# One-hot matrices with the experts innermost and 16-bit operands, and a new order of the operations, in a layer of two mixtures of experts and a state-space scan

## The chip, the cores and the metric

The kernel runs on one core of one Trainium2 chip. The metric is the device time of one execution in microseconds (us), as a median of several runs. The core has five engines that run side by side, each with its own queue of instructions taken in order: TensorE (PE; its weight loads are listed apart as PEld), VectorE (DVE), ScalarE (ACT), GpSimd (POOL) and SyncE (SP), which issues most of the DMAs. An instruction that must wait for another engine holds up everything behind it on its own engine.

## What is computed

The input x has 2 sequences of 2048 positions with 128 features, in float32. Three stages follow one another, each added to x:

```python
x = x + 0.5 * ffn(layernorm(x))     # mixture of experts
x = x + attn(layernorm(x))          # state-space scan
x = x + 0.5 * ffn(layernorm(x))     # mixture of experts, the same weights
```

The mixture `ffn` takes all positions as one flat list of tokens and treats each of them by itself.

```python
scores = softmax(flat @ router_w.T + router_bias)       # 32 experts
topk_scores, topk_idx = top_k(scores, 4)                # normalised to a sum of 1
h = silu(flat @ gate_w[e].T) * (flat @ up_w[e].T)       # per expert e, 128 wide
out = sum over the 4 experts of score * (h @ down_w[e].T)
out = out + (silu(flat @ sgate_w.T) * (flat @ sup_w.T)) @ sdown_w.T   # shared, 512 wide
```

The scan `attn` computes, from the 128 features, 256 channels u, z and dt and 16-wide B and C per position, and then for each position t in order

```python
h = h * exp(dt_t * A) + (dt_t * u_t) * B_t     # 256 channels x 16 states
y_t = sum over the states of h * C_t  + D * u_t
```

followed by `y * silu(z)` and a projection back to 128 features. Position t needs the state of position t-1, so the blocks of one sequence follow one another.

## The kernel before

The 4096 positions are 8 blocks (`NBLK`) of 512 (`T`), four to a sequence; a block is a tile of 128 partitions x 4 (`TB`) x 128. Blocks 0 to 3 are one sequence, 4 to 7 the other. Each mixture is done in four groups of blocks (`GROUPS`, line 37): in the first layer blocks (0), (1), (2, 3), (4 to 7), in the second (0 to 3), (4, 5), (6), (7). The text names them M00 to M03 and M10 to M13, and the scans of the blocks S0 to S7.

**A group of several blocks** sorts its tokens by expert with indirect DMAs: POOL writes ("scatters") each token's row four times, once for each of its experts, into a table in HBM (L964), the experts' quads read it back, and POOL fetches ("gathers") the four results of every token (L1347). Behind every third such DMA in a row a POOL memset of `pad` (L406) lets time pass.

**A group of one block** (M00, M01, M12, M13; `fixed` in the code) sorts without DMAs. The token rows are split in three 16-bit parts (`xp`), and a one-hot matrix `oh` says which token stands in which place of which expert's tile of R rows (`ROWS`: 96 rows, in M13 112). `loc` (L1010) holds for each token and expert the place within that expert's tile; `marks` (L1159) compares it with the numbers 0 to R-1 in `iota_s`, two of the four token tiles at a time; `sorted_rows` (L1173) multiplies, 12 matmuls a quad, into the PSUM tile `pt_x`. A group has 8 quads of 4 experts (`SQ`), so 16 `marks` and 96 such matmuls. Then, for all groups alike, ACT copies `pt_x` to `xT` (L1184), PE makes gate and up (`gu`, L1192), ACT the silu (L1204), DVE the product `h` (L1210), PE the down product (`oq`, L1220), ACT copies it to `yq` (L1229), SP stores it. After the last quad of a group stands the operation `more` on all engines (L1275): a branch that is not taken when all tokens found place. Behind it come the gathers and their weighted sum into x (`joined`, L1372, or matmuls, L1404).

**The scan** of a block has 16 steps, one for each state: POOL makes the driving term (L1630), ACT two decays (`da`, L1642), DVE two scans over 512 positions (L1668) and the product with C (L1681), PE turns and sums (L1445).

**The order.** Every piece of work is declared with `op(engine, cost, function, reads, writes, ...)`, 4233 in all, numbered as they are declared. `Plan.run` does not plan: it takes the order written out in the string `ORDER`, and checks it against the dependences and against the rings of buffers (`RINGS`). The operations are emitted in that order, so each engine's queue follows from it. `tables` (L410) loads another function table on ACT (L412) wherever a silu follows an exponential in this order or the reverse: 140 such loads before.

```python
for part in ORDER.split():
    first, _, last = part.partition("-")
    order += [self.ops[i] for i in range(int(first), int(last or first) + 1)]
```

The weights of the experts are read from the inputs once, in M00, and laid into `w_dram` in HBM from there; rows of tables that may stay unwritten are cleared at the start (L478).

Of the kernel before, what the change touches and what calls it, by code (L numbers as in the profile page):

```python
# [9 lines left out]
BF16 = mybir.dt.bfloat16  # L10
# [38 lines left out]
0 93-96 3 492 97-98 2 10 8 120 491 493 9 121-122 99-101 264 494 102-106 123 495-496 108 107 109 497 11 110-111 13 12  # L49
557 559 558 560 112 561 563 124 113 562 262 16 29 23 564 116 500 114 177 565 60 567 1 115 117-118 566 568 266-267 50  # L50
24 501-502 14 42 119 182 569 571 498 503 268-269 504 499 19 18 570 59 181 505-506 183 273 64 21 572 274 164 28 573 165
179 300 507-508 47 275 509 184 301 166 37 72 145 574 510 65 27 55 511 167 30 302 512 25 40 143 125 127 185 514 513 45
186-187 20 515 86 126 128 516 129 270 160 22 131 130 188 26 271-272 15 517 189 17 525 529 551 265 132 147 548 58 190
148 550 69 518 133 135 263 276 134 136 149 277 180 199 137 150 521 144 168 198 162 139 138 171 169-170 554 215 140
172-173 216 200-201 519-520 191 535 178 154-155 141 522 192 156 303 523 7 5 524 575 211 304 142 228 819 577 6 151 305
152 161 306-307 576 153 174 327 53 175 579 233 578 194 217 278 581 196 580 52 213 4 532 232 218 157-158 308 583 44 57
821 556 193 820 31 582 250 249 205 214 328 585 206-207 163 555 542 547 584 309 546 549 202-203 586-587 234 204 534 589
176 235 310 543 146 526 311-312 247 230 588 590 818 536 822 552 823 208 591-592 540 209 197 313-314 316 332 537 334
219 222 210 553 220-221 333 528 545 223-224 335 315 239 317-318 240 245 241 251 319-320 323 252 212 225 824 336 195
226 527 338 256 159 539 76 257 54 258 337 339 236-238 340 342 253 324 538 341 533 254-255 343 325 231 242 246 531 56  # L60
243 229 530 248 344 244 331 259 227 46 260-261 345-346 279 825 36 347 834 348 541 39 326 544 829 826 91 930 932 43 292
329 349 931 830 290 831 933-934 428 827 330 41 936 828 935 835 937 836 938 832 352 427 940 839 833 939 941 353 321 942
322 34 943 33 49 944-945 840 837-838 841 35 593 842 48 843-846 848 850 849 847 851 85 32 350 298 282 285 852-853 855
854 856-858 63 429 51 283 351 354-355 38 288 649 430 398 395 425 431-433 281 61 75 410 396 287 356 397 357 412 291 413
358 426 411 399 359-361 434 400 435-436 367 297 368 414-415 437 404-405 438 362 296 406 366 458 363 419-420 439 74
369-370 401-402 421 280 293 284 416 68 295 457 417-418 365 403 459-460 407 286 866 408 885 455 371-373 380 461-462 867
422 456 364 409 463 423 79 90 878 374-375 442 376-377 381 440 83 594 382 464 82 378 383 441 465 384-385 289 294 859
893 389-390 466 876 424 467 896 386 468 299 443 877 873 892 747 387 391 62 444 388 596 1395 595 445 597 886 446-447
1396 875 449-450 874 887 451 448 598 601-603 607 599 868 872 890 379 600 392-393 469 650 652-654 1397 651 608 80 895
869 897 894 452 81 453 677 880 891 889 879 881 655-656 604-605 657-659 609 882 862 888 863 1398-1402 84 883-884 870  # L70
1404 394 454 470 678-679 1403 871 1405 1415-1416 1421-1424 1417-1418 660-661 1419 1425 680-682 489 685 1420 610 748
473 476 683 1426 918 903 684 686 611 687 77 1408 78 1409-1413 750-751 864 662 615-616 1429 1414 617 749 755 92 1431
1430 1427 688 483 471 1433 612 1432 689 1434 663 613 606 756 67 757 752-753 1439-1440 614 1435 1441 618 666 1449 1436
905 481 1459 619 1443 667 1442 664 754 758 668 691 1444-1445 1450 472 482 1460 665 929 912 1451 636 669 692 690 1437
759 1452 1454 1446 1455 1453 1456 1461 635 1428 1438 1448 638 1447 671 1464 1463 1462 1465 1469-1470 1479 670 1457
1466 694 1471 693 1472 695 734 637 474 639 672 1474 640-641 487-488 1473 720 673-674 1481 1458 620 642 1475 643 1476
910 1482 1468 675 696-697 733 736 66 1480 1484-1485 1483 1467 1491 719 1478 1489 698 1492 1486 644 1493 1477 479 486
478 475 1499 737 760 645 1406 1490 920 699 1407 700 1494-1495 738 646-647 739 1496 1501 477 1487 621 484 904 480
701-702 676 1502 740 703 722-723 1500 1504 1488 1511 1505 485 724 721 725-726 1497 735 741 909 914 922 921 727-728
1503 1506 1509 705 742-743 1519 490 1510 1513-1514 1512 729 1498 648 706 744 708 1521 745 1599 73 71 1515 70 1600 704  # L80
730 1516 709 1508 1518 917 926 906 928 622 1522 1520 1524-1525 731 1601 1523 1529 1602 761 707 713 1603 732 1526 710
714 1533 711-712 746 899 915 900 913 1531-1532 715 860-861 624-625 1530 1604 626 623 1507 1539 908 1605 627 629 924
902 1534-1535 1003-1004 630 628 716 1017 631 898 1528 1540 1549 1517 1608-1609 923 919 1559 927 916 717 1541 1073 632
1542 633 1550 1536 718 1538 1537 865 1543 901 1610 1606-1607 1611 1544 1551 1545-1546 1612-1613 1615-1616 1554 1553
1018 1527 907 1614 1552 925 911 634 1569 1555 1625-1626 1617-1618 1561 1031 1627 1560 1619 1548 1562 1628 1556 88 1016
1002 1570 1563 1620 762 1564 1621-1622 1629 1030 1558 1557 1019 1571 1565 1005 1547 1623-1624 1074 1020 1072 1574 1021
1032 1572 1006 1010 1024 1022 1566-1567 1579 771 1573 1023 1086 1011 1025 1012 1075-1076 766 1580 769 1033 764 1034
1633 1026 1044 1007-1008 1575 1077-1078 1576 1009 1079 1027 1581 1058 1643 1028 1013-1014 1630 1038 1080 1045 1035
1584 89 1583 1568 1039-1040 1081 1029 1082 786 1036-1037 1059 1046-1047 1582 1585 1048 1635 1634 1083-1084 1041-1042
1061 1089 1586 765 1636 1090 1062 1101 1060 1644 1100 1638 1087 1639 1578 1049-1051 773 1052 1066 1102 1053 1067 763  # L90
1015 1103 1054 1068 1645 1637 1653 1640 1648 1646 1577 1104 772 1588 1055-1056 1649 1088 1663 767-768 770 1085 1655
1091 1114-1115 1092 1647 1063-1064 1093 1065 1650 1108 778 1654 1589 1594 1109 1094 1105 776 1587 783 1631 1043 1095
1106 1656 806 1110 1673 1657 1069 1664 1128 1096 1683 1107 1057 1658-1659 1070 1651 777 1665 1097-1098 1117 1632 780
1118 1641 1660 1111 1131 1642 1112 1666 779 784 1667 1132 1156 1668-1669 774-775 1675 785 1116 1142 1159 1119 1129
1071 1122 1160 1157 1130 1670 1661 1120 1123 1652 1693 781 787 1671 1121 1674 1143 1158 1124 1677 788 1678 1145 782
1676 789 1803 1146 1804 1685 1703 1595 1662 1596 1144 1805 1679 1684 1688 1184 1680 1125 1694 1185 1136 793 1126 1686
1133 1164 1713 807 1672 1689 1704 1165 1723 1134 1687 1137-1138 1682 1695 1166 1806-1807 1186 1696 1135 1690 1150 1161
1810 1127 1198 1099 1698-1699 1162 1151 1811 1692 1681 1697 1152 1163 1705 1590 1706 1139 1187 1140 1188 1691 1700
1591 1701 1113 1714 1733 1708 1167 1702 1709 791 1724 1707 1710 1715 1168 1141 1718 1808 1170 1192 1171 87 1716 1147
1809 798 1743 1193-1194 799 1201 1717 1173 1734 1148-1149 1199 1719-1720 1816 1725 1728 1727 1712 1202 1726 1817 1819  # L100
1153 800 1172 1820 1174 1753 1729 1203 1722 1735 1821 1154 1736 1822 1721 804 1204 792 1178 1763 1730 1738 1731 1205
1179 1737 1180 1200 1206 1711 1207 1739 1189-1190 1175 1732 1176 1745 1208 1740 1191 1744 1754 1177 1748 1829 1746
1749 1747 1830 1818 1773 1755 797 1831 1758 1756 790 1750-1751 1741 1832 1759 1592 1226 1593 1764 1169 1765 1823-1824
1742 1212 805 1757 1752 1195 1213 1783 1254 1766 1825 1227 1768 1760 1214 1826 801 1597 1774 1767 1833 1837 1784 1761
1155 1196-1197 1598 1769 1827 1847 1209 1215 1228 1775 1834 1778 794 1210 1776 1857 1762 1181 1216 1182 1779 1770 1785
# [209 lines left out]
def macaron_kernel(  # L315
# [243 lines left out]
    for R in sorted(set(ROWS.values())):  # L559
# [5 lines left out]
        steps_of[R] = cut, head, n  # L565
    iota_s = kept("iota_s", [P, P])
    nc.gpsimd.iota(iota_s.t, [[1, P]], channel_multiplier=0, allow_small_or_imprecise_dtypes=True)
    iota_p = kept("iota_p", [P, 1])
    nc.gpsimd.iota(iota_p.t, [[0, 1]], channel_multiplier=1, allow_small_or_imprecise_dtypes=True)


# [1258 lines left out]
```

## Time and profile before

| | |
|---|---|
| time before, median of 3 runs (lowest to highest) | 1249.62 us (1238.38 to 1252.58) |
| the profiled execution: its own time | 1252.94 us |
| its span, from the first to the last instruction | 1251.2 us |
| mean granted TensorE clock | 0.899 of full speed |
| busy: PE, DVE, POOL, ACT | 950.7, 931.3, 903.8, 751.8 us |
| `marks`, all 64 | 61.7 us of DVE |
| function table loads, 140 | 179.6 us of ACT, 1283 ns each |

"Busy" is the time in which an engine ran an instruction. The page's second part cuts the span into 40 slices of 31.3 us and gives the busy share of each in tenths. A group of instructions is listed with its line, engine, operation, tiles (written<-read), shapes, count, busy time and mean duration, and behind the bar the idle time of its engine just before these instructions and what ended it. A wait is put down to the engine whose work came last.

### The profile page before, as it was taken

How to read it: one execution, taken by the hardware profiler on the slowest of the kernel's cores; microseconds unless marked ns; L12 is line 12 of the kernel's file. 1: busy time of each engine (PE TensorE's matmuls, PEld its weight loads, DVE VectorE, ACT ScalarE, POOL GpSimd, SP SyncE). 2: the span in 40 equal slices, each digit the busy share in tenths (PEclk: the TensorE clock that was granted, in tenths of full speed). 3: DMA queues.
4: the chain of work that ended last, by engine and by line, in shares of the span. 5: the costliest groups of instructions: out<-in, count | busy, mean ns of one | idle time of the engine just before them, and what ended most of it. 6: DMA issues, size and time to landing. Idle time of an engine off the chain costs nothing. (4 is left out here: it accounts for less than half of the span.)

```text
span 1251.2 us, 18918 instructions
## 1 busy us (share of the span) xinstructions
PE 950.7 (76%) x5752; PEld 730.4 (58%) x5752; DVE 931.3 (74%) x1798; ACT 751.8 (60%) x1390; POOL 903.8 (72%) x917
## 2 busy tenths in 40 slices
PE   5978687666779898776878735757787887899883
PEld 3756465456578686454646524544576766677552
DVE  7863853289678899999999999998873465776533
ACT  4443324685879899977898755646676553533120
POOL 0483584588777786899979788888638476778576
PEclk9998889797889999998998877777899998999987
DMA  9884766394679764232432312223499767766432
GB/s 305 279 257 160 214 191 187 107 289 157 197 236 280 222 196 135 69 84 59 101 77 62 79 52 74 82 86 87 139 309 283 217 210 227 241 194 192 144 99 68
DMA packets 211117, 207.93 MB, mean 166 GB/s; under 512 B 21697, under 2 KB 179522, under 8 KB 210978
## 3 DMA queue, kind: packets, MB, share of 16 engines
q1 hardware_dynamic: 196642, 176.92, 46.9%
q0 software_dynamic: 14336, 29.39, 8.2%
q8 instruction: 59, 0.97, 0.3%
q14 instruction: 80, 0.66, 0.2%
HBM read 146.26 MB, written 59.97 MB: 165 GB/s over the span
## 5 line engine op out<-in xcount | busy, mean ns | idle before, releaser
L1630 POOL TENSOR_TENSOR hst<-dtu,bs 128x1024 f32<-128x1024 f32 x128 | 302.6, 2369 | 90.2 <-DMA bs<-bd 30.1
L1347 POOL DMA_INDIRECT yg<-ys,idx x192 | 190.0, 990 | 93.7 <-issue 37.7
L1668 DVE TENSOR_TENSOR_SCAN hst<-da,st,hst 128x512 f32<-128x512 f32 x192 | 240.2, 1272 | 23.5 <-ACT da L1642 10.3
L1192 PE MATMUL gu<-xT,wt 128*128 128x128 f32 (+2 forms) x1536 | 209.9, 289 | 40.8 <-DMA wt<-w_dram 9.7
L1192 PEld LDWEIGHTS gu<-xT,wt 128*128 128x128 f32 x1536 | 196.3, 202 | 65.2 <-issue 29.9
L1642 ACT ACTIVATE da<-dt,a 128x512 f32<-128x512 f32 x256 | 174.5, 689 | 79.4 <-DVE hst L1668 73.9
L1445 PEld LDWEIGHTS y<-ident,hst 128*128 128x128 f32 x1024 | 133.9, 156 | 108.3 <-issue 78.1
L1445 PE MATMUL y<-ident,hst 128*128 128x128 f32 x1024 | 150.3, 298 | 46.6 <-DVE hst L1681 44.8
L964 POOL DMA_INDIRECT xs<-xn,idx x128 | 128.2, 1002 | 77.9 <-DVE hs L1045 44.3
L1210 DVE TENSOR_TENSOR h<-sgq,gu 128x256 f32<-128x256 f32 (+2 forms) x192 | 72.9, 396 | 146.4 <-ACT sgq L1204 79.9
L412 ACT ACT_TABLE_LOAD x140 | 179.6, 1283 | 3.3 <-PEq L1818 0.8
L1681 DVE TENSOR_TENSOR hst<-hst,c 128x1024 f32<-128x1024 f32 x128 | 154.7, 1209 | 5.1 <-PE c L1654 2.2
L1204 ACT ACTIVATE sgq<-gu 128x256 f32<-128x256 f32 (+2 forms) x192 | 67.2, 367 | 120.0 <-PE gu L1192 76.8
L1220 PE MATMUL oq<-wt,h 128*128 128x128 f32 (+2 forms) x768 | 115.4, 298 | 27.0 <-DVE h L1210 12.6
L1220 PEld LDWEIGHTS oq<-wt,h 128*128 128x128 f32 (+2 forms) x768 | 102.3, 200 | 48.3 <-DVE h L1210 14.2
L1184 ACT COPY xT<-pt_x 128x512 f32<-128x512 f32 (+2 forms) x96 | 52.9, 555 | 81.5 <-PE pt_x L1173 39.3
L1229 ACT COPY yq<-oq 128x512 f32<-128x512 f32 (+2 forms) x96 | 55.8, 582 | 67.8 <-PE oq L1220 45.4
L1654 PE MATMUL c<-cm,pick 128*128 128x512 bf16 x128 | 53.4, 417 | 51.5 <-DVE hst L1681 48.3
L1347 POOL DMA_INDIRECT yg<-xs,idx x64 | 65.4, 1023 | 33.8 <-issue 21.1
L406 POOL MEMSET pad<- 128x256 bf16 x268 | 87.9, 328 | 0.2
L1668 DVE TENSOR_TENSOR_SCAN hst<-da,hst 128x512 f32<-128x512 f32 x64 | 75.6, 1211 | 12.1 <-POOL hst L1630 7.0
L964 POOL DMA_INDIRECT xs<-dtu,idx x64 | 65.4, 1023 | 24.5 <-DVE idx L880 13.0
(175 smaller groups left out, 1636.0 us busy)
## 6 DMA issues: line engine op xcount, KB each, us to landing
wt<-w_dram SPq DMA_DIRECT2D x256, 192.0 KB
bs<-bd SPq DMA_DIRECT2D x128, 256.0 KB
xs<-xs SPq DMA_DIRECT2D x64, 256.0 KB
wt<-w_dram SPq DMA_DIRECT2D x32, 384.0 KB
xs<-zero SPq DMA_DIRECT2D x40, 256.0 KB
ys<-yq SPq DMA_DIRECT2D x40, 256.0 KB
w_dram<-wt SPq DMA_DIRECT2D x16, 384.0 KB
xs<-yq SPq DMA_DIRECT2D x24, 256.0 KB
```

Source lines behind the costliest of these rows:

```text
L406: pool(nc.gpsimd.memset(pad, 0.0))
L412: nc.scalar.preload_act_table_set(name)
L964: nc.gpsimd.indirect_dma_start(out=xs_b.t, out_offset=bass.IndirectOffsetOnAxis(ap=route["idx"][:, i * TB + t, k : k + 1], axis=0), in_=xn ...
L1192: nc.tensor.matmul(gu.t[:, j, s, :], wt.t[:, s, j * H : (j + 1) * H], xT.t[:, s0 + s, :], start=True, stop=True,)
L1210: lambda h=h, s0=s0, sg=sg, gu=gu: nc.vector.tensor_tensor(h.t[:, s0 : s0 + 2, :], sg.t, gu.t[:, 1, :, :], ALU.mult),
L1220: nc.tensor.matmul(o.t[:, s, :], h.t[:, s, :], wts[s // 2].t[:, s % 2, 2 * H :], start=True, stop=True,)
L1347: nc.gpsimd.indirect_dma_start(out=yg.t[:, k, :], out_offset=None, in_=ys_t, in_offset=bass.IndirectOffsetOnAxis(ap=route["idx"][:, i * TB ...
L1445: nc.tensor.matmul(y[:, t, k * P : (k + 1) * P], src[:, k, t * P : (t + 1) * P], ident.t, is_transpose=True, start=start and k == 0 and t ...
L1630: nc.gpsimd.tensor_tensor(h.t[:, :, 1:], dtu.t, bs.t.unsqueeze(1).to_broadcast([P, ND, T]), ALU.mult)
L1642: nc.scalar.activation(da.t, dt.t[:, k, :], AF.Exp, scale=a_t.t[:, k, s : s + 1])
L1668: nc.vector.tensor_tensor_scan(h.t[:, k, 1:], da.t, h.t[:, k, 1:], 0.0 if ini else st_sb[:, k, s : s + 1], ALU.mult, ALU.add,)
L1681: nc.vector.tensor_tensor(h.t[:, :, :T], h.t[:, :, 1:], cb.t.unsqueeze(1).to_broadcast([P, ND, T]), ALU.mult,)
```

## The change

The one-hot matrix is laid out anew. In `oh` the four experts of a quad are now the innermost dimension and the rows stand outside them (`[P, TB, P, SQ]` in place of `[P, TB, SQ, P]`). The numbers that `loc` is compared with come from a new 16-bit constant `rows_s`, 4 equal numbers for each row, written once by POOL at the start; `loc` itself is written as 16-bit. So both operands of `marks` are bf16 and run with step 1 over the innermost four, where before both were f32 and the second stood still over the innermost R. The matmuls of `sorted_rows` therefore give their columns by row and then expert; the tile `pt_x` is kept in that order, and ACT's copy to `xT` now reads it with a step of 4 elements, to write the same `xT` as before. The `more` branch keeps the old layout.

`ORDER` is replaced throughout. Its numbers name the same 4233 operations.

```diff
 ORDER = """
-0 93-96 3 492 97-98 2 10 8 120 491 493 9 121-122 99-101 264 494 102-106 123 495-496 108 107 109 497 11 110-111 13 12
+...
-...
+4088-4090 4216 4221 4226 4231-4232
 """
...
+    rm = max(ROWS.values())
+    rows_s = kept("rows_s", [P, rm, SQ], BF16)
+    nc.gpsimd.iota(
+        rows_s.t, [[1, rm], [0, SQ]], channel_multiplier=0, allow_small_or_imprecise_dtypes=True
+    )
...
-            xp, loc = buf("z", [P, 3, TB, D], BF16, name="xp"), buf("loc", [P, TB, E])
+            xp = buf("z", [P, 3, TB, D], BF16, name="xp")
+            loc = buf("loc", [P, 2, TB, E], BF16, part=lambda t: t[:, 0])
...
-            px = buf("w", [P, SQ, R], name="pt_x")
+            px = buf(
+                "w", [P, SQ, R], name="pt_x",
+                part=(lambda t: t.rearrange("p s r -> p (s r)").rearrange("p (r s) -> p s r", s=SQ))
+                if fixed else None,
+            )
...
-                oh = buf("dt", [P, TB, SQ, P], BF16, name="oh", part=lambda t: t[:, :, :, :R])
+                oh = buf("dt", [P, TB, P, SQ], BF16, name="oh", part=lambda t: t[:, :, :R, :])
...
                         nc.vector.tensor_tensor(
                             oh.t[:, t0 : t0 + 2],
-                            iota_s.t[:, :R].unsqueeze(1).unsqueeze(1).to_broadcast([P, 2, SQ, R]),
+                            rows_s.t[:, :R, :].unsqueeze(1).to_broadcast([P, 2, R, SQ]),
                             loc.t[:, t0 : t0 + 2, q * SQ : (q + 1) * SQ]
-                            .unsqueeze(3)
-                            .to_broadcast([P, 2, SQ, R]),
+                            .unsqueeze(2)
+                            .to_broadcast([P, 2, R, SQ]),
                             ALU.is_equal,
                         )
...
                             nc.tensor.matmul(
-                                px.t,
+                                px.t.rearrange("p s r -> p r s"),
                                 xp.t[:, j, t, :],
                                 oh.t[:, t],
```

## The prediction

> **What bounds the kernel now.** I read the page's slices first, then its stretches, then who waits for the operation that the change makes faster, last the chain at the end. The slices, each 31.3 us:
>
> ```profile
> PE   5978687666779898776878735757787887899883
> DVE  7863853289678899999999999998873465776533
> ACT  4443324685879899977898755646676553533120
> ```
>
> DVE is full from slice 11 to slice 28: there the scans run. Before and behind it DVE is half idle and PE is fuller. So I cut the span at the first scan (246 us), at the first scan of the last block (848) and at its last one (1030), and asked for each engine's busy time in each stretch (columns: stretch, length, then busy us and count of PE, PEld, DVE, ACT, POOL, and last the clock, DMA share and GB/s):
>
> ```profile
> 0.00:246.00 246.00, 183.94 (x1012) 132.06 (x1013) 140.54 (x483) 104.31 (x205) 126.65 (x196) 0.90 0.68 213
> 246.00:848.00 602.00, 444.62 (x2671) 346.02 (x2670) 544.98 (x765) 467.46 (x863) 507.19 (x369) 0.89 0.46 134
> 848.00:1030.00 182.00, 146.68 (x981) 120.24 (x980) 119.14 (x211) 115.10 (x186) 118.32 (x130) 0.93 0.69 210
> 1030.00:1252.00 222.00, 175.49 (x1093) 132.09 (x1091) 126.59 (x340) 64.97 (x137) 151.59 (x225) 0.91 0.57 167
> ```
>
> The opening is 246 us with DVE idle for 105; the scans are bound by DVE (545 of 602); the last 222 us by PE more than by DVE, which is idle for 95. Now `marks`, by shape, and the answer for its line on who waited for it:
>
> ```profile
> L1159 DVE TENSOR_TENSOR oh<-iota_s,loc 128x768 bf16<-128x768 f32 x48 | 44.8, 948 | 0.0
> L1159 DVE TENSOR_TENSOR oh<-iota_s,loc 128x896 bf16<-128x896 f32 x16 | 16.9, 1085 | 1.4 <-issue 1.0 <-PE pt_x L1173 0.3
> ```
> ```profile
> who waited for it (us, times):
>   PE pt_x L1173: 0.9, 1
> ```
>
> All 64 lie in the two outer stretches, 32 in each, where DVE has room. Only once, for 0.9 us, did PE wait for one. What a shorter `marks` can give must come through the DVE instructions queued behind it.
>
> **Part 1, the faster comparison.** The two shapes give its price: 128 elements more take 137 ns more, 1.07 ns an element, with 948 - 768 x 1.07 = 126 ns fixed. The trace of before has no DVE product of two 16-bit operands, so I bound it: at worst nothing is gained (948 and 1085 ns stay; more elements or bytes are not moved, so no loss); at best two elements go where one went, 126 + 411 = 537 and 126 + 479 = 605 ns. I take the best end, because the shapes' rows say that four fifths of the duration is per element; it saves 0.41 us and 0.48 us: 32 x 0.41 = 13.2 us of DVE in the opening, 16 x 0.41 + 16 x 0.48 = 14.3 us in the last stretch, none in between.
>
> [...]
>
> How much of it is on the path? It can give no more than what PE waits for DVE behind the first `marks`. The waits of PE between 28 and 246 us that name DVE, the longest of them:
>
> ```profile
> PE tot L791 <- DVE mk L779: 8.3, 1, 8.3
> ...
> PE gu L1192 <- DVE x L1068: 4.4, 1, 4.4
> ...
> PE pt_x L1152 <- DVE ea L1584: 3.7, 1, 3.7
> PE oq L1220 <- DVE h L1210: 3.1, 3, 1.3
> ```
>
> With `h` for `gu` (1.0) and `oh` (0.9) that is 21.4 us. Before the 8.3 us DVE runs the routing of M03, with four `marks` among it from 126 to 133 us (4 x 0.41 = 1.6), but much of that stretch is itself a wait for PE's `up`; `ea` has no `marks` ahead of it. I take 4 us of the 13.2. In the last stretch PE waits for DVE 4.1 (`oq` for `h`) + 3.5 and 2.9 (for x L1372) + 1.5 (`hs`) = 12.0 us; the x of L1372 wait for gathers, so mainly the `h` can shrink: 3 us of the 14.3. Ends: 0 and 13.2, 0 and 12.0. Nothing covers what is left over: it becomes idle time of DVE.
>
> **Part 2, the copy.** ACT now reads `pt_x` with a step of 16 bytes, 32 times (480 ns for 384 elements before). No row shows a strided read of PSUM. The nearest is DVE's strided write `mk` (L779): 304 ns at 128 elements, 1.24 us at 512 with the wider step, where a plain 512 takes 0.69. So between 0 and as much again, 32 x 0.5 = 16 us of ACT, which is idle for 142 us of the opening and 157 of the end; but PE waits 10.4 (weight loads) and 7.7 us (matmuls) for all 96 copies together, so a third of the worst case, 5 us, would come through. I take 0. `rows_s` is one more iota on POOL (iota_s took 227 ns for 128 elements, so about 0.8 us), at 2 to 3 us, when POOL then sits idle until 48 us: nothing. `sorted_rows` keeps its counts and streams.
>
> **Part 3, the order.** I set the two orders side by side, engine by engine. The stages keep their places. Adding up the DVE durations of this trace along each queue (neighbours overlap a little, so the sums exceed busy time): from the first scan of S0 to the last of S6 584.2 us of DVE work before and 587.7 after; within S7 131.5 and 126.8; behind the last scan 160.4 and 148.6, of which 14.3 is part 1. So DVE's queue changes by about 1 us between the first scan and the last. On PE one `gate_up` and one `down_q` of M02 leave the stretch ahead of the first scan: eight matmuls each, 1.03 + 1.04 = 2.1 us. Behind the last scan PE has two `gate_up`, a shared `gp` and one turned y more, about 5 us, and SP and DVE nothing of weight. On POOL seven scatters of M02 now stand behind M00's first gathers; those wait for `more` (until 116 us before), so the scatters land 10 us later on a POOL that before sat idle twice, 19.6 and 13.0 us, and their rows are first used by PE at 193 us. Hidden; without that cover it would be 10 us. On SP the first weights of M00 stand behind about 3 MB more of loads and clears (twelve transfers of 256 KB); at the 373 GB/s of the second ten us they land 8 us later. Before they are issued from 3.4 us on and first used by PE's `gu` at 33.5 us, so I take 0 of the 8.
>
> The function table loads rise from 140 to 152: +1 ahead of the first scan, +7 in S0 to S6, +6 in S7, -2 behind. A load and the next instruction:
>
> ```profile
> 223.41 1.28 ACT L412 ACT_TABLE_LOAD   x1
> 224.71 0.58 ACT L1577 ACTIVATE ps_dt<-ps_dt 128x512 f32<-128x512 f32 x1
> ```
>
> so 12 x 1.283 = 15.4 us of ACT. [...] Here the next instruction starts 0.02 us behind the load, so the trace decides for 1.283. Between 246 and 848 ACT is idle for 134 us, 74 of them (over the whole run) waiting for DVE to free a buffer of its decays; the loads fit into that, and I cost them at 0.
>
> What else the new order does with single waits cannot be counted. Downward: DVE idles between 246 and 848 for `h` on ACT 12.4 us, for POOL's driving term 11.4, for decays 8.9, without a named cause 7.8, for `cm` 3.5: 44 us; half of it gone would be -22. Upward: all twelve loads on the path, +15.4. I take -2, the PE work that left the opening, since it is the only row that I can count.
>
> **Sum:** -4 - 3 - 2 = -9 us, so 1252.94 - 9 = 1244 us for an execution like the profiled one. That one lies 3.3 us above the median of the runs, 1249.62; the median so becomes **1240.6 us**, 0.7% less.
>
> **Rivals.** (a) *Nothing gets through:* the 0.9 us that PE waited for `oh` speaks for it, the waits of 21.4 and 12.0 us against. Then 1249.6, and with the copy's 5 us 1255. (b) *The order gives more:* part 1 at its ends, -13.2 - 12.0, or half of DVE's scan waits, -22, with the -9: 1249.6 - 31 = 1219 to 1228. For it: 57 us of DVE idle time in the scans; against: the same work stands between the same scans. (c) *Slower, by the table loads:* in S0 to S7 ACT runs 41 to 47 of 50 us between 350 and 500 us, and DVE already waits for its decays; a load put directly ahead of a decay delays a scan by 1.28 us. All 13 that are new from S0 to S7: +16.7 with nothing gained, 1266 us. It becomes slower by over 1% once ten of them (12.8 us) are on the path. [...]
>
> **How the numbers follow.** A measurement of this kernel can tell about 1% from no change: 1237.1 to 1262.1 is "same". The forecast's own range is 1229 to 1246 and has 0.5, of which 0.22 lie below 1237; (a) and (d) 0.15; (b) 0.15; (c) 0.20. So faster 0.37, same 0.43, slower 0.20. The range takes in most of (b) and all that (c) gives up to ten or so loads: 1217 to 1265; two in ten are left out.
>
> **What would show it.** Right: `marks` at about 540 and 605 ns; the copy of 384 elements still at 480; 152 loads at 1283 ns; the first scan near 241 us and the stretch from there to the last scan within 5 us of 783. Wrong: `marks` unchanged; copies near 700 ns; DVE's idle time for decays above 8.9 us by tens (c); the first scan before 232 us or the scan stretch shorter by over 15 (b). If the opening shrinks but the end does not move, the gain was given back to PE.

## The result, and the profile after

| | before | after |
|---|---|---|
| median (lowest to highest), same chip | 1250.03 us (1238.38 to 1252.58), 4 runs | 1261.37 us (1255.05 to 1269.13), 4 runs |
| ratio, with its 95% interval | | 1.0117 [1.0067, 1.0166] |
| the profiled execution: its time, its span | 1252.94, 1251.2 us | 1255.05, 1253.3 us |
| `marks`, all 64 | 61.7 us | 35.9 us |
| table loads | 140, 179.6 us | 152, 195.0 us |

The change made the kernel slower by 1.2%. The profiled execution of after is its fastest, that of before its slowest, so the two traces differ by only 2 us; what they show is where time moved. The slices of after (31.3 us each):

```profile
PE   5988777575789888677786756656787877999874
DVE  6854742487578899899999999987775355774443
ACT  4544325787789798878798856636757653542220
```

DVE is less busy at the start, as forecast. Slices 15 to 27, all at 9 before, now hold an 8 at 17 and at 27, and 28 to 30 show 7, 7, 7 for 8, 8, 7: while the scans run, DVE is less full. The stretches, cut at the same places of the work as in the prediction (columns: stretch, length, busy us and count of PE, PEld, DVE, ACT, POOL, then clock, DMA share and GB/s):

```profile
0.00:239.00 239.00, 184.90 (x1011) 132.94 (x1011) 128.80 (x483) 105.16 (x206) 123.95 (x197) 0.92 0.71 220
239.00:856.00 617.00, 448.04 (x2684) 349.92 (x2684) 540.81 (x772) 477.84 (x871) 508.63 (x376) 0.89 0.45 128
856.00:1037.00 181.00, 142.71 (x936) 116.77 (x935) 108.26 (x201) 118.23 (x185) 118.26 (x131) 0.93 0.70 213
1037.00:1253.00 216.00, 175.67 (x1125) 134.90 (x1125) 114.56 (x343) 67.57 (x141) 147.30 (x225) 0.93 0.59 174
```

The opening is 7 us shorter, the last stretch 6. In the second line, from the first scan on, the scans S0 to S6 take 617 us where they took 602, with *less* DVE work (541 for 545): DVE stands idle there for 76 us instead of 57. `marks`, ACT's copy and the table loads, by shape:

```profile
L1170 DVE TENSOR_TENSOR oh<-rows_s,loc 128x768 bf16<-128x768 bf16 x48 | 26.2, 559 | 3.1 <-PE pt_x L1184 1.0 <-PE gp L1037 0.9 <-issue 0.8
L1170 DVE TENSOR_TENSOR oh<-rows_s,loc 128x896 bf16<-128x896 bf16 x16 | 9.7, 618 | 1.2 <-PE pt_x L1184 1.2
L413 ACT ACT_TABLE_LOAD x152 | 195.0, 1283 | 3.6 <-PEq L1829 0.8
L1195 ACT COPY xT<-pt_x 128x384 f32<-128x384 f32 x24 | 11.4, 477 | 36.7 <-PE pt_x L1184 21.6 <-PE oq L1231 7.1 <-remote 3.8
```

The comparison is as fast as estimated (559 and 618 for 537 and 605 ns), and the copy with its step of four elements costs what it cost (477 for 480 ns). What DVE waited for in the second stretch, before (246 to 848 us) and after (239 to 856 us): who waits and for whom, us in total, times, the longest:

```profile
DVE h L1210 <- ACT sgq L1204: 12.4, 11, 3.2
DVE hst L1668 <- POOL hst L1630: 11.4, 8, 4.3
DVE hst L1668 <- ACT da L1642: 8.9, 13, 1.7
...
DVE hst L1681 <- PE c L1654: 2.2, 3, 1.8
```
```profile
DVE hst L1679 <- POOL hst L1641: 23.7, 18, 3.6
DVE h L1221 <- ACT sgq L1215: 14.5, 15, 3.6
DVE hst L1679 <- ACT da L1653: 9.8, 13, 2.2
DVE hst L1692 <- PE c L1665: 4.0, 8, 0.8
DVE z L1746 <- PE pz L1735: 3.7, 1, 3.7
...
DVE x L1426 <- PE sum L1415: 2.2, 2, 2.0
```

The scans' wait for POOL's driving term has doubled (+12.3 us), and four others (for `sgq`, `c`, `pz`, `sum`) have grown by 2 to 4 us each; the wait for `cm` (3.5 us before) is gone. The decays (`da`), by which the forecast's rival (c) would show, account for 0.9.

Of the 12.3 us, 9.4 fall into S0 (2.7 to 12.1 us), a block that now begins earlier: the scans of its first state end at 242.1 us for 252.7, those of S1's at 363.6 for 368.2. From there to the same point of S7 it takes 493.3 us where it took 482.9, and in this part the wait for POOL has hardly grown (7.5 to 8.5 us).

### The profile page after: what moved, and what is told of

Same layout as the page of the kernel before. It is cut to its first block, busy times and chain, and to the rows that moved or that the text cites. A ratio compares the mean times of both kernels' runs of the same rounds, so it can differ in the third digit from the quotient of the medians.

```text
span 1253.3 us, 18990 instructions
## 1 busy us (share of the span) xinstructions
PE 951.3 (76%) x5752; PEld 734.5 (59%) x5752; DVE 892.4 (71%) x1798; ACT 768.8 (61%) x1402; POOL 898.1 (72%) x926
## 5 line engine op out<-in xcount | busy, mean ns | idle before, releaser
L1679 DVE TENSOR_TENSOR_SCAN hst<-da,st,hst 128x512 f32<-128x512 f32 x192 | 239.6, 1272 | 23.2 <-POOL hst L1641 11.4
L1203 PE MATMUL gu<-xT,wt 128*128 128x128 f32 (+2 forms) x1536 | 215.7, 294 | 45.8 <-issue 12.9
L1203 PEld LDWEIGHTS gu<-xT,wt 128*128 128x128 f32 x1536 | 200.8, 206 | 72.5 <-issue 23.3
L413 ACT ACT_TABLE_LOAD x152 | 195.0, 1283 | 3.6 <-PEq L1829 0.8
L1692 DVE TENSOR_TENSOR hst<-hst,c 128x1024 f32<-128x1024 f32 x128 | 155.1, 1212 | 13.6 <-remote 5.9
L1231 PE MATMUL oq<-wt,h 128*128 128x128 f32 (+2 forms) x768 | 110.1, 290 | 13.4 <-DVE h L1221 8.2
L407 POOL MEMSET pad<- 128x256 bf16 x276 | 90.9, 329 | 0.2
L1358 POOL DMA_INDIRECT yg<-xs,idx x64 | 62.2, 972 | 29.5 <-DVE x L1383 13.5
L1037 PE MATMUL gp<-xnT,w_all 128*128 128x512 f32 x128 | 72.0, 646 | 13.2 <-issue 8.0
```

The source lines that it names most:

```text
L407: pool(nc.gpsimd.memset(pad, 0.0))
L413: nc.scalar.preload_act_table_set(name)
L1203: nc.tensor.matmul(gu.t[:, j, s, :], wt.t[:, s, j * H : (j + 1) * H], xT.t[:, s0 + s, :], start=True, stop=True,)
L1231: nc.tensor.matmul(o.t[:, s, :], h.t[:, s, :], wts[s // 2].t[:, s % 2, 2 * H :], start=True, stop=True,)
L1358: nc.gpsimd.indirect_dma_start(out=yg.t[:, k, :], out_offset=None, in_=ys_t, in_offset=bass.IndirectOffsetOnAxis(ap=route["idx"][:, i * TB ...
L1679: nc.vector.tensor_tensor_scan(h.t[:, k, 1:], da.t, h.t[:, k, 1:], 0.0 if ini else st_sb[:, k, s : s + 1], ALU.mult, ALU.add,)
```

## The experiments

**Theory Q** (called O in the first four expectations): the new order costs the time, through waits of DVE between the first scans of S0 and S5 that it had not before. **Rivals:** L, the twelve added table loads cost it; the layout costs it (called L, too, in the first two expectations); P and C, what a faster comparison gives is lost in the outer stretches, where PE and the clock it is granted set the pace.

The kernel before takes 1204, 1246, 1268 and 1272 us on the other chips that these runs got, so only ratios to it on the same chip are compared, and stretches that depend on the chip only within a chip. Since the operations are the same, any two orders can be joined wherever the dependences and rings of buffers allow it. The table has the medians' ratios and, from each one's profiled execution, the time up to the scans of S0's first state ("opening"), from there to the same point of S7, then to S7's last scan, and the rest of the span.

| kernel | before on its chip | ratio [95%] | opening | S0 to S6 | S7 | rest |
|---|---|---|---|---|---|---|
| before / after (the result) | 1250 | 1.0117 [1.0067, 1.0166] | 252.7 / 242.1 | 598.4 / 614.9 | 178.1 / 179.8 | 222.0 / 216.6 |
| marks_only | 1204 | 0.9951 [0.9924, 0.9979] | 231.7 | 597.9 | 163.6 | 207.0 |
| order_only | 1204 | 1.0133 [1.0087, 1.0179] | 220.7 | 617.0 | 166.2 | 209.4 |
| ends_new | 1204 | 0.9947 [0.9919, 0.9975] | 221.5 | 610.4 | 164.0 | 198.2 |
| mid_new | 1204 | 1.0133 [1.0086, 1.0180] | 229.6 | 614.4 | 164.9 | 203.8 |
| marks_relu | 1272 | 1.0676 [1.0610, 1.0742] | 268.2 | 585.3 | 273.0 | 227.8 |
| after_relu | 1272 | 1.0780 [1.0731, 1.0830] | 263.7 | 610.1 | 265.0 | 240.3 |
| win_s2_s4 | 1272 | 1.0205 [1.0152, 1.0258] | 272.6 | 614.5 | 187.9 | 228.0 |
| win_s5_s6 | 1272 | 1.0119 [1.0064, 1.0173] | 268.2 | 595.9 | 188.0 | 234.3 |
| before_same_chip | 1246 | one time, 1245.3 us | 247.7 | 597.5 | 180.0 | 218.4 |
| after_same_chip | 1246 | 1.0106 [1.0072, 1.0141] | 240.7 | 617.6 | 177.0 | 219.1 |
| marks_same_chip | 1246 | 1.0022 [0.9992, 1.0051] | 251.0 | 596.7 | 179.2 | 226.1 |
| ends_same_chip | 1246 | 1.0035 [0.9998, 1.0072] | 242.3 | 608.7 | 177.8 | 223.8 |
| marks_twice | 1268 | 1.0250 [1.0205, 1.0295] | 268.0 | 597.4 | 186.6 | 246.5 |
| loads_28 | 1268 | 1.0132 [1.0089, 1.0175] | 256.1 | 607.4 | 187.0 | 231.6 |
| s2_old | 1268 | 1.0186 [1.0134, 1.0237] | 263.3 | 608.4 | 179.1 | 243.2 |
| one_move | 1268 | one time, 1295.6 us | 262.8 | 617.2 | 180.8 | 233.2 |
| marks_third | 1246 | 1.0057 [1.0018, 1.0097] | 254.5 | 590.6 | 181.0 | 220.6 |
| layout_f32 | 1246 | 0.9992 [0.9957, 1.0027] | 244.2 | 600.4 | 177.9 | 218.0 |

(The last two are a further chip, 1245.75 us.)

### 1. The layout alone, the order alone, and the order by halves

```diff
 marks_only: the code of after
-ORDER = new
+ORDER = old
 order_only: the code of before
-ORDER = old
+ORDER = new
 ends_new: the code of after
-ORDER = new
+ORDER = new up to S0's first scan, old up to S7's first scan, new behind it
 mid_new: the code of after
-ORDER = new
+ORDER = old up to S0's first scan, new up to S7's first scan, old behind it
```

> The new layout of the comparisons (experts innermost, 16-bit operands, the strided copy) with the order of before kept as it was. Theory O (the order costs the time, between the first and the last scan): this kernel gains the forecast's parts 1 and 2 alone, 1240 to 1247 us against 1250. Theory L (the layout costs it, by the strided copy or by a clock that falls when PE is fed faster): 1255 to 1263. By both the comparisons take about 559 and 618 ns.

> The layout of before with the order of after. Theory O: the order's loss without the layout's gain, 1264 to 1272 us. Theory L: 1245 to 1250, as the forecast's part 3 alone. Under both the table loads are 152.

> The new layout; the order of after up to the first scan of S0 and from the first scan of S7 on, the order of before in between (144 table loads). Theory O with the loss between the scans S0 to S6: 1238 to 1246 us, so faster than before. If the loss lies in the opening or in the tail instead: 1252 to 1263.

> The reverse: the new layout; the order of before up to the first scan of S0 and from the first scan of S7 on, the order of after in between (148 table loads, the eight new ones all in S0 to S6). Theory O with the loss between the scans: 1254 to 1264 us. If the loss lies at the ends: 1238 to 1246.

The ratios fall in two pairs: the old order in the middle gives 0.995, the new one 1.013, whatever the ends and the layout are. So the order of the middle costs 1.8%, some 20 us by the medians and 16.5 us by the stretch S0 to S6 (597.9 to 614.4). mid_new's 1.0133 is a little above its expectation (at most 1264 us for 1250, 1.011). Of the 16.5 us, 13.4 arise behind S1's first scans, which end at 346.9 and 347.9 us. The order of the ends is worth nothing. The opening does get 10 us shorter with it (231.7 to 221.5); but S0 to S6 then takes longer by 12.5, although the order there is the old one: 4.2 of it in S0, and 6.5 in S6, where the order is cut.

### 2. Without table loads, and where in the middle

```diff
 marks_relu, after_relu
-SILU = "silu_and_others"
+SILU = "natural_log_exp_and_others"
-AF.Silu
+AF.Relu
 win_s2_s4: marks_only's
-ORDER = old
+ORDER = old up to S2's first scan, new up to S5's first scan, old behind it
 win_s5_s6: likewise, from S5's to S7's first scan
```

> Left out: the SiLU. Every Silu is a Relu, which needs no function table of its own, so that no table is switched; else this is marks_only (new layout, order of before). It gives the price of its 139 switches: fully hidden 1196 us as marks_only, fully on the path 1196 - 139 x 1.283 = 1018. I expect 1110 to 1170. It is the base for after_relu.

> Left out: the SiLU, as in marks_relu; else the changed kernel, its order included. Against marks_relu this is the order's cost without any table switches. Theory L (the twelve added table loads cost the time): equal to marks_relu within 5 us. Theory Q (the order of the queues costs it by its waits, loads or not): 12 to 22 us above marks_relu.

> marks_only, but with the order of after from the first scan of S2 up to the first scan of S5. By the stretches of marks_only and mid_new (S2 +6.7, S3 +1.3, S4 +2.7 us) 1204 to 1211 us if theory Q holds and the loss is here. By theory L the three loads that are new here give 4 us: 1200 at most.

> marks_only, but with the order of after from the first scan of S5 up to the first scan of S7. By the stretches of marks_only and mid_new (S5 -1.7, S6 +3.5 us) 1195 to 1200 us under either theory (two new loads); more than 1204 would mean that the loss is not where the stretches of single executions put it.

With the Relu one table load is left (1283 ns in marks_relu). The time as a whole went up, where I had expected 1110 to 1170 us, for a reason of its own: the branch `more`, skipped otherwise, runs 112 matmuls, presumably since the changed values send more rows past the fixed tiles, and S7 takes 273 us. Up to S7 the pair is clean: 585.3 with the old order, 610.1 with the new one. **Without any table switch the new order still costs 24.8 us** there (14 us by the medians); theory L as the cause has fallen. Of the 24.8 us, 12.5 fall into S0, which begins 4.5 us earlier, 6.4 into S1 and 2.8 into S2: other blocks lose than with the switches (section 3). Against win_s5_s6, which has the old order up to S5 on the same chip, 88 loads fewer gained 10.6 us, 0.12 us a load, far from 1.283.

win_s2_s4 puts S2 to S4 at 231.4 us where the old order has 216.5 (win_s5_s6): +14.9 (7.9 of it in S2), where theory Q had 10.7; by the medians it is 10.1 us slower than win_s5_s6. The new order in S5 and S6 costs nothing there (175.6 us; the old order has 174.7 in marks_relu and 175.5 in marks_only). But win_s5_s6's ratio is 1.012, not below 1, and win_s2_s4's 1.021, not 1.000 to 1.006. Since S0 to S6 take 595.9 us in win_s5_s6, as with the old order elsewhere, the miss must lie in the outer stretches; no profile of the kernel before was taken on this chip. That led to the next runs.

### 3. Everything on one chip

> The kernel before, unchanged, for a profile from the same chip as the next three runs, since absolute times differ between the chips seen so far (1204, 1250, 1272 us for the kernel before). Ratio to itself 1.00 within 0.5%.

> The changed kernel, unchanged, beside its parts. Theory Q (the order loses 15 to 22 us of waits between the scans, wherever it runs): 1.008 to 1.018 of the kernel before, and the stretch from the first scan of S0 to the first of S5 13 to 18 us longer than in before_same_chip. If the chip decides (theory C): a ratio outside of this.

> The kernel of marks_only again (new layout, order of before). Theory Q: 0.992 to 0.998 of the kernel before on this chip too, the stretch of the scans S0 to S4 within 2 us of that in before_same_chip. Theory C (on a chip that grants a lower clock the faster comparison gives nothing or costs, as win_s5_s6 with 1.012 may hint, whose order is that of before up to S5): 1.003 to 1.015.

> The kernel of ends_new again (order of after only outside of the stretch S0 to S6). Theory Q: 0.990 to 0.998, so a version faster than both. Theory C: 1.003 to 1.015, as marks_same_chip.

(Kernels as above, with no new edit.) The result repeats: 1.0106. S0 to S6 is 20.1 us longer than before; the opening is 7.0 shorter, S7 3.0, the rest 0.7 longer. By block, S0 to S6 before: 114.9, 88.7, 78.2, 67.6, 70.8, 93.2, 84.1 us; after: 121.4, 91.0, 87.4, 68.9, 72.5, 89.1, 87.3. S0 and S2 lose most, but S0 only gives back what the opening gained: S1's first scans end at 362.6 us before and at 362.1 after. From there to S7's it takes 13.6 us longer (482.6 to 496.2), 9.2 of it in S2.

marks_same_chip puts the new layout at 1.0022, not below 1: the scans are as before (596.7), the opening is 3.3 us *longer* and the rest 7.7. So the shorter opening of after is the order's, not that of `marks`, and ends_same_chip shows how it is lost: its first scans end at 242.3 us, 5.4 before those of before, and S1's first at 362.6, the same as before (362.6). What holds S0 seems to be POOL, whose last scatter of M03 comes no earlier (327.8 for 328.1 us).

Two places of after show the new waits. In S0 POOL puts scatters and gathers between the driving terms, nearly as many in all as before (47 for 48), but before up to four at a time, now up to five at some places and two at others:

```profile
318.88 2.36 POOL L1641 TENSOR_TENSOR hst<-dtu,bs 128x1024 f32<-128x1024 f32 x1
321.41 1.01 POOL L970 DMA_INDIRECT xs<-dtu,idx  x1 [0.17 <-issue]
322.72 0.97 POOL L970 DMA_INDIRECT xs<-dtu,idx  x1 [0.30 <-issue]
323.69 0.33 POOL L407 MEMSET pad<- 128x256 bf16 x1
...
328.09 2.36 POOL L1641 TENSOR_TENSOR hst<-dtu,bs 128x1024 f32<-128x1024 f32 x1
```
```profile
317.24 0.41 DVE L1221 TENSOR_TENSOR h<-sgq,gu 128x256 f32<-128x256 f32 x1
321.28 2.34 DVE L1679 TENSOR_TENSOR_SCAN hst<-da,hst 128x512 f32<-128x512 f32 x2 [3.62 <-POOL hst L1641]
```

(The timeline of after: start, duration, engine and line; in brackets the idle time before.) The driving term starts at 318.9, behind a row of scatters, and the scan that needs it waits 3.62 us; the next one comes 9.2 us later, behind five more scatters. Before, with four between them, the two that follow each other at about this time were 7.7 us apart:

```profile
325.71 2.36 POOL L1630 TENSOR_TENSOR hst<-dtu,bs 128x1024 f32<-128x1024 f32 x1
...
333.44 2.38 POOL L1630 TENSOR_TENSOR hst<-dtu,bs 128x1024 f32<-128x1024 f32 x1
```

That these longer runs cost the time is not shown. No run moves them alone, and ends_same_chip, with the old order from S0's first scan on, waits 7.0 us for POOL in S0 too, where before_same_chip waits 0.6 and after_same_chip 10.1: an S0 that begins earlier finds POOL no earlier.

In S2 (after_same_chip) it is a chain through three engines:

```profile
471.95 2.08 PE L1478 MATMUL ps<-xnTs,win 128*128 128x512 f32 x2 [2.79 <-DVE hst L1692]
473.81 1.91 PE L1203 MATMUL gu<-xT,wt 128*128 128x128 f32 x8
```
```profile
474.06 0.69 ACT L1489 ACTIVATE z<-ps,bin 128x512 f32<-128x512 f32 x1 [4.41 <-PE ps L1478]
475.83 0.38 ACT L1215 ACTIVATE sgq<-gu 128x256 f32<-128x256 f32 x1 [1.08 <-PE gu L1203]
```
```profile
476.24 0.42 DVE L1221 TENSOR_TENSOR h<-sgq,gu 128x256 f32<-128x256 f32 x1 [3.32 <-ACT sgq L1215]
477.90 0.29 DVE L1426 TENSOR_TENSOR x<-x,sum 128x128 f32<-128x128 f32 x1 [1.24 <-PE sum L1415]
```

The next block's projection `ps` waits on PE, by the profile for DVE's product with C, and a `gate_up` of M03 now stands behind `ps`. PE idles 2.8 us, the silu is late, and DVE, whose queue has `h` ahead of the next scan, idles 3.3. Before, three `gate_up` stood ahead of this `ps`; their silu ran in a row, and DVE made the three `h` without a wait (before_same_chip):

```profile
474.67 1.05 DVE L1210 TENSOR_TENSOR h<-sgq,gu 128x256 f32<-128x256 f32 x3
```

### 4. The price of DVE's time and of a table load; one block and one link undone

```diff
 marks_twice: the kernel before
 def marks(q=q, t0=t0, oh=oh):
-    nc.vector.tensor_tensor(...)
+    for _ in range(2):
+        nc.vector.tensor_tensor(...)
 loads_28: the kernel before
 def decay(s=s, k=k, da=da, b=b):
+    if k == 0 and s % 4 == 2 and b < 7:
+        loaded[0] = None
     tables(EXP)
 s2_old: the code of after
-ORDER = new
+ORDER = new up to S2's first scan, old up to S3's first scan, new behind it
 one_move: the code of after
-... 1871 1865 ... 1812 1276 1813 1277 ...
+... 1276 1277 1871 1865 ... 1812 1813 ...
```

> The kernel before with every comparison issued twice: 32 x 948 ns = 30.3 us more of DVE in the opening, 16 x 948 + 16 x 1085 ns = 32.5 us more in the last stretch. By the forecast's share for part 1 (a quarter of a saved microsecond reaches the end) about +16 us, a ratio of 1.013. Theory P (the two outer stretches are held by PE and the clock that it is granted, DVE's time there is spare): -2 to +5 us, 0.998 to 1.004. If DVE's time were all on the path: +63, 1.05.

> The kernel before with a superfluous table load ahead of the first decay of four states in each of the blocks S0 to S6, 28 in all, 35.9 us of ACT. Rival (c) of the forecast (a load ahead of a decay delays its scan by 1.28 us): +25 to +36 us, 1.020 to 1.029. By marks_relu, where some 75 loads fewer shortened S0 to S4 by 9.7 us, 0.13 us a load: +4 us, 1.003. The twelve of the changed kernel would then account for 1.5 of its 11 us.

> The changed kernel with the order of before in one block alone, S2 (300 of 4,233 operations stand elsewhere; the table loads stay 152). Theory Q: S2 goes from 83.6 to 87.4 us in the runs with the new order back to 78.2, and the whole to 1.002 to 1.006 of before instead of 1.011. Theory L (loads) or a loss that only moves on: 1.009 to 1.013.

> The changed kernel with two operations moved, the second gate_up of slot group 19 of M03 and its silu: on PE's and ACT's queues from behind S2's third projection (which waits on PE for DVE's product with c) to ahead of it, as the kernel before has them. By theory Q the wait of 3.3 us of DVE's h at the fifth state of S2 goes, and S2 becomes 2 to 3.5 us shorter than in s2_old's counterpart after_same_chip (87.4); the whole moves by 0 to 3 us, too little for one time to tell.

- **marks_twice** costs 2.5%, some 31 us for the 62.8 us of DVE added, none of it in S0 to S6 (597.4). So half of an added microsecond reaches the end, twice the forecast's share; that DVE's time there is spare (theory P) is refuted for time added.
- **loads_28** has 162 loads, 22 more than before. S0 to S6 takes 607.4 us, 10.0 more than in marks_twice: 0.45 us for each of the 22. The ratio of 1.013, between what the two theories had, is 16.7 us; the other 6.7 would be in the outer stretches, where no load was added and no profile of the kernel before shows them on this chip. By 0.45 the eight new loads in S0 to S6 are 3.6 us of the 16 to 20.
- **s2_old:** S2 takes 79.2 us, where one_move on the same chip has 86.0, and S0 to S6 608.4 for 617.2: 8.8 us come back with the order of one block, 6.8 of them in that block, the table loads being still 152. The ratio did not come down to 1.006: after itself was not run on this chip, and the outer stretches are long here (opening 263.3). So the gain stands in single profiles; the whole time, 1292.0 us for the one time of one_move of 1295.6, does not show it.
- **one_move** took that wait away, and S2 took 86.0 us, within the 83.6 and 87.4 us of after and after_same_chip. DVE's waits in S2, of after_same_chip and of one_move:

```profile
DVE x L1426 <- PE sum L1415: 4.1, 3, 1.9
DVE h L1221 <- ACT sgq L1215: 3.9, 3, 3.3
```

```profile
DVE hst L1692 <- PE gu L1203: 3.0, 1, 3.0
DVE x L1426 <- PE sum L1415: 2.8, 2, 1.9
...
DVE h L1221 <- ACT sgq L1215: 0.6, 2, 0.4
```

`h` waits 0.6 us for the silu in place of 3.9, but now the product with C waits 3.0 us, by the profile behind a `gate_up`. My single link is not what costs S2 its time; which part of the block's order does is not shown.

### 5. The layout without the faster comparison

```diff
 layout_f32: marks_only's code and order
-            loc = buf("loc", [P, 2, TB, E], BF16, part=lambda t: t[:, 0])
+            loc = buf("loc", [P, TB, E])
```

> The kernel of marks_only once more (new layout with 16-bit operands, order of before), beside layout_f32 on the same chip. By marks_only and marks_same_chip 0.992 to 1.005 of before; if the chip is one on which the kernel before takes 1268 us or more, win_s5_s6 lets expect 1.005 to 1.015.

> As marks_third, but the ranks (loc) stay 32-bit, as in before: the new layout with its strided copy, and comparisons that should take the old 948 and 1085 ns, since one operand is 32 bits wide. Theory P (DVE's time in the outer stretches is spare at the margin, what a faster comparison gives goes to idle time): equal to marks_third within 0.3%. If the faster comparison does give its share (the forecast's 7 us): 0.4 to 0.8% above marks_third. If feeding PE faster costs clock: below marks_third. If the layout itself costs (strided copy, order of the streamed columns): both above 1.003.

The answers for the line of `marks`, of layout_f32 and of marks_third (count, shortest, median and longest ns):

```profile
L1169 DVE TENSOR_TENSOR oh<-rows_s,loc x64: 925/952/1094, 26.6 to 1181.5; 128x768 bf16<-128x768 bf16 x48, 128x896 bf16<-128x896 bf16 x16
```
```profile
L1169 DVE TENSOR_TENSOR oh<-rows_s,loc x64: 526/552/637, 26.6 to 1187.0; 128x768 bf16<-128x768 bf16 x48, 128x896 bf16<-128x896 bf16 x16
```

With one operand of 32 bits the new layout keeps the old duration, 952 ns in the median for 951 before; with both of 16 bits it takes 552. Whether 16-bit operands in the old layout would be as fast, no run shows.

The layout by itself costs nothing: 0.9992. And the kernel with the *slow* comparison is the faster of the two, 1242.8 us against 1251.1 (the two intervals just overlap): the comparison that saves 26 us of DVE gives nothing here, and by the medians loses 0.7%. The windows up to 180 us, to 200 and to 240 us, of layout_f32 and of marks_third, columns as above:

```profile
0.00:180.00 180.00, 143.93 (x835) 102.74 (x835) 123.45 (x445) 73.61 (x149) 96.56 (x160) 0.94 0.77 243
180.00:200.00 20.00, 14.13 (x108) 12.04 (x108) 6.12 (x21) 10.62 (x24) 16.99 (x26) 1.00 0.83 254
200.00:240.00 40.00, 23.07 (x80) 15.69 (x81) 12.08 (x18) 20.67 (x35) 17.27 (x14) 0.74 0.34 104
```
```profile
0.00:180.00 180.00, 140.96 (x795) 99.78 (x795) 105.31 (x423) 70.65 (x143) 89.14 (x155) 0.93 0.74 234
180.00:200.00 20.00, 13.49 (x63) 10.84 (x64) 10.04 (x33) 5.01 (x10) 17.68 (x28) 0.66 0.60 184
200.00:240.00 40.00, 28.15 (x149) 20.64 (x147) 9.73 (x22) 23.02 (x43) 11.54 (x13) 0.87 0.40 115
```

From 180 to 200 us PE did 108 matmuls at a granted clock of 1.00 in layout_f32, and 63 at a granted 0.66 in marks_third. There PE first waited 2.98 us for an `h`; behind the wait eight `gu` matmuls took 1.86 us where layout_f32's took 1.03. That the wait brought the lower clock is not shown.

Nor do these 20 us account for the difference. At 180 us marks_third is already 40 matmuls behind, from 200 to 240 us its clock is the higher one (0.87 for 0.74), and at 240 us it is 16 behind (1007 for 1023). That the faster comparison moved PE's pauses, and that this took its gain away, is my guess and not shown: the runs show that the time did not fall.

## Why the prediction was wrong

The forecast was 1240.6 us; it became 1261.4, with the wrong sign. That this lies in the range of 1217 to 1265 is luck: its upper end was set for rival (c), whose mechanism it is not.

- **Part 3, the order, taken at -2 us, is the step that failed.** Counted in durations it was near: DVE's busy time between the first scans of S0 and S7 fell by 4 us, where the count had it rise by 3.5. But "I take -2 [...] since it is the only row that I can count" priced the waits at zero. From S1's first scans to S7's the kernel takes 10.4 us longer (13.6 on another chip, 13.4 with the order of the middle alone). And the opening's gain, which the sum carried to the end, was mostly lost in S0: S0's first scans end 10.6 us earlier, S1's 4.6 (on the other chip 7.0 and 0.5). That the order of the middle does this is shown by the runs that exchange it (mid_new, win_s2_s4, s2_old in its block). Which waits make it up differs from block to block and chip to chip: for silu, weighted sums, `pz` and `c` on ACT's and PE's queues behind S0, for POOL's driving term in S0; no single link was shown to be the cause. S0 to S6 as a whole grew by 16.5 us, near the +15.4 that I had put as the upper end, but that was the price of the table loads, so the nearness is chance. I had followed the scatters of M02 into the opening, but had not counted, in the order's text, what stands between two driving terms on POOL, or whose queue each item of DVE's queue depends on.
- **Part 1, the faster comparison, -7 us.** Its duration was right within 4%. That two elements would go where one went was an assumption, which no trace of before showed; with both operands of 16 bits in the new layout the runs show 559 and 618 ns, 0.46 ns for each added element where before it was 1.07. The share on the path differs by chip: -0.5% (6 us, near the forecast) where the kernel before takes 1204 us, +0.2% (an interval that holds no change) and +0.6% on the two where it takes 1246, as rival (a) had it. Time added costs a half, time saved gave nothing on two of three chips, so the quarter that I took has no support as a rule. That PE and its clock hold these stretches is argued, not shown.
- **Part 2, the copy, 0:** right, 477 ns for 480, and 0.9992 for the layout.
- **The marks that I set.** The first scan near 241 us: 239, but for another reason, the order of the opening; with the old order and the new layout it came at 244.5 us on one chip, where the kernel before has 240.6. The scans' stretch within 5 us of 783: wrong, 15 us longer. "If the opening shrinks but the end does not move, the gain was given back to PE": in S0, whose scans wait for POOL, and then to DVE's waits. One reading was loose: DVE's slices 11 to 14, called full, show 6, 7, 8 and 8.
- **Rivals.** (c), slower, had the right sign and the wrong mechanism: DVE's wait for decays rose by 0.9 us, by 0.45 us each the loads explain some 4 us, and without any load the order still costs 24.8 us in S0 to S6. (b) had no support; (d), a comparison that is no faster, was false: 559 and 618 ns for 948 and 1085.

No version was found that beats the kernel before on every chip: the best, ends_new and marks_only, gain 0.5% on one chip and nothing, or lose, on others.

## What to carry to other kernels

When an order is replaced, the sum of durations on each queue need not show the cost, as here; what is worth counting in the new order is, for each item on the bounding engine's queue, how far ahead its producer stands on its own queue, and what stands between (here a silu behind a projection that itself waits, or POOL's DMAs between two driving terms). An earlier start was worth nothing where the next block waited for something that came no earlier (ends_same_chip: S0's first scans 5.4 us earlier, S1's none). An engine with idle time can charge for time that is added without paying for time that is saved, as DVE did for `marks` (some 31 us for 62.8 added, on two of three chips no gain for 26 saved). Joining two orders at places where the state of the buffers is the same finds the guilty stretch in two or three runs, and a stretch bound by one engine (S0 to S6 with the old order, the silu and no added load: 597 to 600 us in six of seven profiles, 590.6 in the seventh, on at least four chips) tells more than the whole time.

## What the runs showed of the hardware

- The same kernel took 1204 to 1272 us on different chips. S0 to S6, where DVE is busy for 545 of 602 us before, hardly differs with the order of before and its silu (590.6 to 600.4 us); the outer stretches do: one and the same program had its first scans done at 231.7, 251.0, 254.5 and, with the same order up to there, 268.2 us, at granted clocks of 0.92, 0.90, 0.90 (up to 244 us) and 0.87.
- In single profiles a superfluous table load cost 0.45 us in the scans, a load taken away gave 0.12, at 1.283 us each: the price of a load beside the bound was not one number.
